# Deformable convolution and attention, fp32, one core: the totals' adds moved two slots forward, the first loads of an image on another queue, and key and query room lent to the last prefetches

## The chip, the cores and the metric

The kernel runs on one core of one Trainium2 chip. A core has five engines with instruction streams of their own, each in order: TensorE (PE; PEld is its weight load), VectorE (DVE), ScalarE (ACT), GpSimd (POOL) and SyncE (SP). Transfers between DRAM and on-chip memory are issued by SyncE, ScalarE and GpSimd, each on a queue of its own, and are carried out by 16 DMA engines that all queues share. The metric is the device time of one execution in microseconds, as the median of several runs. A profiled execution gives the span from its first to its last instruction, and a trace of every instruction.

## The reference

Two layers work on `x` of 2 images x 512 channels x 64 x 64 pixels, all fp32. Layer 0 is a deformable convolution (group norm, offsets and masks, bilinear samples, output projection, residual). It takes the first third of the time, and the change doesn't touch it. Its result `x1` goes into layer 1:

- a group norm of `x1` gives the input of the attention, 4096 pixels of 512 channels per image;
- queries and keys have 64 channels each, q = tanh(Wq x) scaled by a vector, k = tanh(Wk x); values are v = Wv x;
- attention: softmax over all 4096 keys of k.q, for each of 4096 queries; the result is the values' mean under these weights;
- the normalised input is added (a residual inside the attention), the output projection Wfc with bias follows;
- a batch norm over both images and all pixels, with ReLU, and `x1` is added at the end.

Since the batch norm needs the mean and variance of everything, nothing of the output can be stored before the last product is done.

## The kernel before

Layer 1 is written at L1242 to L1807. The order of the instructions on each engine is the order in the code (`tc.manual_schedule()`); no scheduler moves anything.

**Algebra.** Wv and Wfc are merged, so that the values come out already projected. The softmax isn't normalised first: e = exp(scores) is multiplied with the values, all e are summed over the keys ("totals"), and the product is multiplied by the reciprocal of the total at the end. The residual is multiplied by the total beforehand, so that one division serves both. The product of values and e is a two by two block product that uses seven products instead of eight (`ORDER`, L1487), and each of the seven is once more cut in the same way into seven matmuls. So sums and differences of the factors are needed: "forms" of the values (`vform`, `vsum`), made once per image on VectorE, stored to DRAM by SyncE (L1341, L1342) and loaded again as `v`, 448 KB for each slot (L1473); rows of e that become sums of each other (L1387, L1419, L1420); and three block sums `tt` (L1466, L1467) for each slot.

**Loops.** An image has four chunks of 1024 queries (two rows of 512, "row 0" and "row 1"). A chunk has seven products (p), and each sums over nine groups (g): eight groups of 512 keys and a ninth for the residual, whose values are a matrix of weights (`w_d`). One product of one group is a slot: seven block products of two matmuls each. A chunk has 63 slots, numbered l from 0 (p = l // 9, g = l % 9), and an image has 252 (s = 63 k + l).

**Order around a slot.** `slot(s)` issues, in this order: the load of `v` for slot s + 3; `before`, which settles the scores of the slot before (transforms e, adds it to totals) and computes new scores and exponentials that `EVENTS` has for this slot; `at`, with the single events of the slot (loads and normalisations of the residual, at 23 the row sum of row 1's total); the sums `tt` of slot s + 4, with exceptions around 4, 20 and 22; the last adds of a total at slots 4 (row 0) and 22 (row 1); the products; and at the end steps of the work that collects an earlier product. From l = 43 the next chunk's scores are computed beside the products. The scores of the last row piece, `e1`, stand at slots 11, 13, 15 and 20.

**Totals.** Each row has two partial totals of 512 KB. The first e is copied into each by GpSimd's DMA (L1415), later ones are added by accumulating DMAs (L1411), to one and the other in turn (`parts.reverse()`). The last two of row 1, groups 6 and 7, are added by VectorE itself (L1409). `total` then adds the two partial totals (L1436) and folds the sum twice (L1437, L1438), and `spread_total` sums over the partitions on TensorE with a matrix of ones (`pr`, L1442), scales the residual by it (L1458) and copies it to `rin`.

**Start of an image.** For each of the four quarters of an image the keys, queries and values are computed (`values`); row 0's early scores of the first chunk are computed between these (`EARLY`). The forms are stored as they become ready, the last of them during slots 0 to 4 (`step(2)`). The first three loads of `v` are issued behind the third tile of the last quarter, on SyncE's queue, which also carries all stores of the forms.

**Room.** `ring` has 38 pieces of 512 KB for e, totals, pixels, results and prefetches; `wk` has keys (1 MB), queries (512 KB), `rin`, `u`, four `v` and five tiles shared by `tt` and `vsum`. After the loop `wk` is closed and `fin` takes ten pieces in its place.

**The end.** For each of 32 pieces of output (an item), `xr` (the piece of x1) and `cr` (the attention's result, which for the last chunk is kept on chip instead) are loaded; ScalarE applies batch norm and ReLU (L1803), VectorE adds (L1806), GpSimd stores (L1807). From slot 28 of the last chunk GpSimd already prefetches items into free ring pieces; after the loop SyncE fetches five more into `fin`, and the rest follows into pieces that come free, as items are done:

```python
live = 6 + sum(last + g >= l for last in (18, 41, 45, 54) for g in range(NG + 1))
if live + 2 * len(ready) + 2 <= 36:
    fetch(piece, nc.gpsimd)
```

Of the kernel before, what the change touches and what calls it, by code (L numbers as in the profile page):

```python
# [10 lines left out]
F32 = mybir.dt.float32  # L11
# [7 lines left out]
P = 128  # L19
NB = 2  # L20
# [11 lines left out]
CH = 512  # L32
NCH = S // CH
# [494 lines left out]
NG = S // P // 4  # L528
SLOTS = 7 * (NG + 1)
# [45 lines left out]
def window_path(ctx: ExitStack, tc: tile.TileContext, t_in: dict, out: bass.AP, far: bass.AP, sums: bass.AP):  # L575
    nc = tc.nc
# [10 lines left out]
    v_d = [[dram.tile([7, P, 7, P], F32, name=f"wv{n}_{g}") for g in range(NG)] for n in range(NB)]  # L587
    w_d = dram.tile([7, P, 7, P], F32, name="ww")
# [54 lines left out]
    with ExitStack() as l0:  # L643
# [298 lines left out]
        def fetch(i, s):  # L942

            if i >= NSEQ:
                return
            n, ch = divmod(i, NCH)
            t = io.tile([P, PX, C], F32, name="patch", bufs=2)
            for p in range(PX):
                nc.sync.dma_start(
                    t[:SN, p, :], xt_d[n][ch * ROWS + PR * s : ch * ROWS + PR * s + SY, PC * p : PC * p + SX, :]  # L950
                )
            patches[i, s] = t
# [208 lines left out]
        with tc.manual_schedule():  # L1161
# [60 lines left out]
            for i in range(NSEQ):  # L1222
# [6 lines left out]
                w, m, g = Chain(weights, i + 1), Chain(sample, i), Chain(features, i + 3)  # L1229
# [12 lines left out]
    with ExitStack() as l1, tc.manual_schedule():  # L1242
# [9 lines left out]
        def piece(name, shape=(P, 2, CH)):  # L1252
            return ring.tile(list(shape), F32, tag="r", name=name)

        kept = {}
        waiting = deque((n, qb, h) for n in reversed(range(NB)) for qb in range(NCH) for h in range(2))
        ready = deque()

# [10 lines left out]
        with ExitStack() as inner:  # L1269
            wk = inner.enter_context(tc.tile_pool(name="w1work", bufs=1))  # L1270
# [88 lines left out]
                yield  # L1359
                finish(odd, 5, 2)  # L1360

            keys = wk.tile([P, NCH // 2, CH], F32, name="keys")

            def load_queries(n, k):
                q = wk.tile([P, 2, CH], F32, name="q")
                for h in range(2):
                    nc.gpsimd.dma_start(q[h * DQ : (h + 1) * DQ], q_d[n][k])
                return q
# [36 lines left out]
            def add_total(c, qh, t, direct=False):  # L1405
                parts = c.tot.setdefault(qh, [])
                if len(parts) == 2:
                    if direct:
                        nc.vector.tensor_add(parts[0], parts[0], t)  # L1409
                    else:  # L1410
                        nc.gpsimd.dma_start(parts[0], t, accum_op=ALU.add)  # L1411
                    parts.reverse()
                else:
                    parts.append(piece("tot"))
                    nc.gpsimd.dma_start(parts[-1], t)  # L1415
# [15 lines left out]
                    if key == "e1":  # L1431
                        second_row(c, k)

            def total(c, qh):
                t, u = c.tot[qh]
                nc.vector.tensor_add(t, t, u)  # L1436
                nc.vector.tensor_add(t[:, 1, :], t[:, 1, :], t[:, 0, :])  # L1437
                nc.vector.tensor_add(t[:, 1, HQ:], t[:, 1, HQ:], t[:, 0, :HQ])  # L1438

# [27 lines left out]
                nc.vector.tensor_add(t[:, 1:3], t[:, 0].unsqueeze(1).to_broadcast([P, 2, HQ]), x[:, 0:3:2])  # L1467
                return t

            def load_values(n, p, g):  # L1470
                j = PLACE[ORDER[p][1]]
                t = wk.tile([P, 7, P], F32, name="v", bufs=4)
                nc.sync.dma_start(t, v_d[n][g][j] if g < NG else w_d[j])  # L1473
                return t

            def products(c, p, g, v, t):
# [80 lines left out]
            class Attention:  # L1557
# [19 lines left out]

                def fetch(self, s):
                    if s < NCH // 2 * SLOTS:
                        self.v[s] = load_values(self.n, *divmod(s % SLOTS, NG + 1))  # L1580

                def at(self, l, c, s):

# [15 lines left out]
                def slot(self, s):  # L1599
                    k, l = divmod(s, SLOTS)  # L1600
                    c = self.chunks[k]
                    nxt = self.chunks[k + 1] if k + 1 < NCH // 2 else None
                    self.fetch(s + 3)
                    if l % (NG + 1) == 0 and self.ends:
                        next(self.ends[-1], None)
                    self.before(l, c)
                    if nxt and l >= 43:
                        if l == 43:
                            nxt.q = load_queries(self.n, k + 1)
                        self.before(l - SLOTS, nxt)  # L1610
                        self.at(l - SLOTS, nxt, s)
                    self.at(l, c, s)
                    if l == 21:
                        self.sums(s + 3)
                    if l + LEAD not in (8, 24, 26):
                        self.sums(s + LEAD)
                    if l in (4, 22):
                        total(c, int(l > 4))
                    p, g = divmod(l, NG + 1)
                    products(c, p, g, self.v.pop(s), self.t.pop(s))  # L1620
                    for e in self.ends[:-1] if g == 0 else self.ends:
                        next(e, None)
                    if g == NG:
                        self.ends = self.ends[-1:] + [collect(c, p, first_copy(c), c.acc)]
# [75 lines left out]
            for n in range(NB):  # L1700
# [3 lines left out]
                for i in range(NCH // 2):  # L1704
# [22 lines left out]
                    for t in range(4):  # L1727
# [17 lines left out]
                        if t % 2:  # L1745
                            g = 2 * i + t // 2
# [8 lines left out]
                for s in range(NCH // 2 * SLOTS):  # L1755
                    if s == 0:
                        at.at(-7, first, s)
                    if s == 2:
                        at.at(-3, first, s)
                    at.slot(s)  # L1760
                    if s < 5:
                        step(2)
                    if n == 0 and s in (92, 94, 96, 98, 101, 103):
                        next(later, None)
                    l = s - (NCH // 2 - 1) * SLOTS
                    if n + 1 < NB:
                        if l == 47:
                            pixels[0] = load_pixels(n + 1, 0, nc.gpsimd)
                        if l == 49:
                            wc = value_output()  # L1770
                        if l == 51:
                            wcs = sum_value_output(wc)
                        if l in (52, 53):
                            for h in range(2):
                                normalize(pixels[0][l - 52][h], 2 * h, *norms[n + 1])
                        if l == 55:
                            psums[0] = sum_pixels(nc.vector, pixels[0])
                    elif l >= 28 and waiting:
                        live = 6 + sum(last + g >= l for last in (18, 41, 45, 54) for g in range(NG + 1))
                        if live + 2 * len(ready) + 2 <= 36:  # L1780
                            fetch(piece, nc.gpsimd)
                at.rest()

        fin = l1.enter_context(tc.tile_pool(name="w1fin", bufs=10, reuse_waits="tile"))
        for _ in range(5):
            fetch(lambda name: fin.tile([P, 2, CH], F32, tag="f", name=name), nc.sync)
        bmv = bnp.tile([P, KB, 2], F32, name="bmv")
        for kb in range(KB):
# [9 lines left out]
        while ready:  # L1798
            n, qb, h, ct, xr = ready.popleft()
# [61 lines left out]
```

## Time and profile before

| | |
|---|---|
| median of 3 runs | 3458.1 us (3456.04 to 3461.37) |
| profiled execution, its own time | 3457.18 us |
| its span | 3455.3 us, granted TensorE clock 0.968 on average |
| TensorE busy | 3159.9 us (91%) |
| VectorE busy | 2757.1 us (80%) |
| ScalarE, GpSimd busy | 1349.8 us, 432.8 us |
| moved by DMA | 629.99 MB, 182 GB/s on average |
| last product of the attention ends | 3361.8 us |

A group in the profile is named by line, engine and "output tile <- input tiles"; a bracket gives the idle time of the engine just before an instruction and what ended it. In the list of waits a row has the total, the number of times and the longest. Windows give the busy time of each engine in a stretch, with the number of instructions, then TensorE's granted clock, the mean busy share of the 16 DMA engines, and GB/s. A busy TensorE is not always at its full clock; a slot's length shows that better.

### The profile page before, as it was taken

The page shows a single profiled execution, that of the slowest core. Times are in us where ns is not written, and L with a number is a line of the kernel's source. Part 1 is how long each engine was busy: PE and PEld are TensorE (multiplying, and loading weights), DVE is VectorE, ACT ScalarE, POOL GpSimd, SP SyncE. Part 2 cuts the span into 40 slices and gives each one's busy share as a digit, 9 for nine tenths or more (in the row PEclk, how much of TensorE's full clock was granted, in tenths as well). Part 3 has the DMA queues.
Part 4 walks back from the last instruction along what each step waited for, and adds up shares of the span by engine and source line. Part 5 has one row for each costly group of instructions (what it writes and reads, how often), then busy time and mean ns, then how long its engine had stood idle before and what let it go on. Part 6 is the DMA issues. An engine that isn't in the chain of part 4 may idle for free. (4 is left out here: it accounts for less than half of the span.)

```text
span 3455.3 us, 38293 instructions
## 1 busy us (share of the span) xinstructions
PE 3159.9 (91%) x14147; PEld 2270.9 (66%) x14147; DVE 2757.1 (80%) x3826; ACT 1349.8 (39%) x1802; POOL 432.8 (13%) x468
## 2 busy tenths in 40 slices
PE   5789999999999999999999999999899999999990
PEld 2355555555555666687787777887577787787780
DVE  8799999989998577786876867868786786876864
ACT  2477787787776533203113122023212203212105
POOL 2112111211211001001001011001001101001012
PEclk9799999999999999999999999999999999999995
DMA  6333442343233279748557677557857748557679
GB/s 224 103 98 129 130 133 88 114 123 117 89 124 98 95 270 278 229 143 245 179 174 218 180 217 205 180 185 254 252 178 218 209 146 244 170 177 211 216 273 375
DMA packets 238390, 629.99 MB, mean 182 GB/s; under 512 B 28112, under 2 KB 45136, under 8 KB 237168
## 3 DMA queue, kind: packets, MB, share of 16 engines
q1 hardware_dynamic: 184048, 439.72, 38.0%
q0 software_dynamic: 43072, 156.26, 17.6%
q10 hardware_dynamic: 11072, 31.46, 2.6%
q8 instruction: 114, 1.87, 0.2%
q14 instruction: 84, 0.69, 0.1%
HBM read 410.15 MB, written 124.91 MB: 155 GB/s over the span
## 5 line engine op out<-in xcount | busy, mean ns | idle before, releaser
L1487 PE MATMUL accy<-tt,v 128*128 128x256 f32 x2016 | 604.5, 382 | 0.1
L1402 ACT ACTIVATE e<-pS 128x1024 f32<-128x1024 f32 x256 | 248.0, 1021 | 736.0 <-PE pS L1397 727.6
L1487 PE MATMUL accx<-e,v 128*128 128x256 f32 x1792 | 477.6, 389 | 27.1 <-DMA v<-wv 27.1
L1487 PE MATMUL accy<-e,v 128*128 128x256 f32 x1792 | 463.1, 381 | 0.0
L820 DVE SCALAR_TENSOR_TENSOR conv<-xn,L_conv_dw_w_sb,conv 128x504 f32<-128x504 f32 (+1 forms) x512 | 409.3, 807 | 35.5 <-ACT conv L814 21.6
L1487 PEld LDWEIGHTS accx<-e,v 128*128 128x128 f32 x1792 | 335.9, 192 | 148.9 <-issue 83.2
L1487 PEld LDWEIGHTS accy<-tt,v 128*128 128x128 f32 x2016 | 386.5, 192 | 54.1 <-issue 0.5
L1487 PEld LDWEIGHTS accy<-e,v 128*128 128x128 f32 x1792 | 343.9, 192 | 48.1
L1466 DVE TENSOR_TENSOR tt<-e 128x256 f32<-128x256 f32 x448 | 187.8, 419 | 185.4 <-PE accy L1487 158.8
L1467 DVE TENSOR_TENSOR tt<-tt,e 128x512 f32<-128x512 f32 x448 | 310.0, 692 | 15.3
L1487 PE MATMUL accx<-tt,v 128*128 128x256 f32 x1008 | 304.5, 384 | 1.1 <-DVE tt L1466 1.1
L984 PEld LDWEIGHTS pa<-bt,patch 96*128 96x128 f32 x2048 | 250.2, 197 | 57.1 <-issue 34.5
L984 PE MATMUL pa<-bt,patch 96*128 96x128 f32 x2048 | 254.1, 281 | 7.3 <-ACT bt L970 6.4
L970 ACT COPY bt<-pb 96x1024 f32<-96x1024 f32 x124 | 234.6, 2007 | 59.6 <-PE pb L965 57.5
L1397 PE MATMUL pS<-q,keys 64*128 64x512 f32 x1024 | 254.4, 615 | 0.0
L789 PE MATMUL pq<-in_w,xn 128*128 128x512 f32 x512 | 240.1, 613 | 6.9 <-DVE o L882 4.8
L1004 PE MATMUL py<-dT,L_conv_out_w_sb 128*128 128x512 f32 x512 | 234.7, 602 | 4.8 <-ACT dT L995 4.8
L1492 ACT COPY u<-accx 128x256 f32<-128x256 f32 x56 | 20.9, 373 | 531.6 <-PE accx L1487 528.8
L1487 PEld LDWEIGHTS accx<-tt,v 128*128 128x128 f32 x1008 | 194.3, 193 | 28.8 <-DVE tt L1466 1.5
L877 PE MATMUL po<-om_w_pg,feat 128*128 128x432 f32 x512 | 204.7, 545 | 2.5 <-ACT feat L860 2.5
L995 ACT COPY dT<-pa 32x256 f32<-32x256 f32 x496 | 179.9, 363 | 62.5 <-PE pa L984 53.7
L1411 POOL DMA_DIRECT2D tot<-e x144 | 124.0, 885 | 582.0 <-DVE e L1387 277.9
(231 smaller groups left out, 4326.0 us busy)
## 6 DMA issues: line engine op xcount, KB each, us to landing
v<-wv SPq DMA_DIRECT2D x448, 448.0 KB
tot<-e POOLq DMA_DIRECT2D x176, 512.0 KB, 6.9
patch<-xt SPq DMA_DIRECT2D x256, 192.0 KB
v<-ww SPq DMA_DIRECT2D x56, 448.0 KB
wv<-vform SPq DMA_DIRECT2D x48, 512.0 KB
wv<-vsum SPq DMA_DIRECT2D x48, 384.0 KB
xt<-xj SPq DMA_DIRECT2D x128, 128.0 KB
res<-in_x SPq DMA_DIRECT2D x64, 256.0 KB
```

The costliest lines, as they stand in the source:

```text
L789: nc.tensor.matmul(pq, xn[:, kb, 1 + 2 * t : 3 + 2 * t, :].rearrange("p r c -> p (r c)"), in_w[:, kb, :], start=(kb == 0), stop=(kb == KB ...
L820: nc.vector.scalar_tensor_tensor(dst, src, wt, dst, ALU.mult, ALU.add)
L877: nc.tensor.matmul(po[:, : 3 * GP], f[:, kb, t * P : (t + 1) * P], om_w[:, kb].rearrange("p a k g -> p (a k g)"), start=(kb == 0), stop=(k ...
L970: copy(bt[:SN].rearrange("s g q d -> s d (g q)")[:, d0 : d0 + 4, :], pb[:SN])
L984: nc.tensor.matmul(pa[:, p], xp[:SN, p, cb * P : (cb + 1) * P], bt[:SN, 4 * cb : 4 * cb + 4, PX * s + p, :], start=True, stop=True,)
L995: copy(dst, src)
L1004: nc.tensor.matmul(py, out_w[:, kb, cb * P : (cb + 1) * P], dT[:, kb, :], start=(kb == 0), stop=(kb == KB - 1))
L1397: nc.tensor.matmul(p[:, a, :], keys[r, i, (2 * u + h) * P : (2 * u + h + 1) * P], c.q[r, qh, :], start=True, stop=True,)
L1402: nc.scalar.activation(e.rearrange("p a q -> p (a q)"), p.rearrange("p a q -> p (a q)"), AF.Exp)
L1466: nc.vector.tensor_sub(t[:, 0], x[:, 1], x[:, 3])
L1467: nc.vector.tensor_add(t[:, 1:3], t[:, 0].unsqueeze(1).to_broadcast([P, 2, HQ]), x[:, 0:3:2])
L1487: nc.tensor.matmul(out, v[:, blk, :], op, start=(first and g == 0), stop=(final and g == NG))
```

## The change

It has three parts.

1. **Totals.** The add of the two partial totals becomes a function of its own, `merge`. For row 1 it is called at the end of slot 20's preparations, and the two folding adds at slot 21, ahead of the `tt` sums of that slot (before: all three at slot 22, behind `tt` sums of slots 21 and 22). `parts.reverse()` now follows accumulating DMAs only, so both direct adds of groups 6 and 7 go into the first partial total, which already holds the sum. Row 0 keeps its three adds at slot 4.
2. **Loads.** The loads of `v` for the first six slots of each image are issued by ScalarE instead of SyncE. By the order of the code, those of slots 0 to 2 stand on ScalarE behind the early exponentials of the last quarter's third tile, those of slots 3 and 4 ahead of the residual's four normalisations, and that of slot 5 behind them.
3. **Room.** Keys and queries move from `wk` to a pool `lent` that stays to the end. From slot 22 of the last chunk of the last image the room of keys and queries, three pieces, takes prefetches, and the limit counts ring pieces that were really taken instead of two per item. After the loop SyncE fills the ring up to 34 pieces; `fin` has eight pieces instead of ten and takes four items instead of five.

```diff
@@ -1252,7 +1252,12 @@
         def piece(name, shape=(P, 2, CH)):
             return ring.tile(list(shape), F32, tag="r", name=name)
 
-        kept = {}
+        lent = l1.enter_context(tc.tile_pool(name="w1lent", bufs=1))
+        kept, taken = {}, []
+        def ring_piece(name):
+            taken.append(name)
+            return piece(name)
+
         waiting = deque((n, qb, h) for n in reversed(range(NB)) for qb in range(NCH) for h in range(2))
         ready = deque()
 
@@ -1359,10 +1364,16 @@
                 yield
                 finish(odd, 5, 2)
 
-            keys = wk.tile([P, NCH // 2, CH], F32, name="keys")
+            def key_tile():
+                return lent.tile([P, NCH // 2, CH], F32, tag="keys", name="keys")
+
+            def query_tile():
+                return lent.tile([P, 2, CH], F32, tag="q", name="q")
+
+            keys = key_tile()
 
             def load_queries(n, k):
-                q = wk.tile([P, 2, CH], F32, name="q")
+                q = query_tile()
                 for h in range(2):
                     nc.gpsimd.dma_start(q[h * DQ : (h + 1) * DQ], q_d[n][k])
                 return q
@@ -1409,7 +1420,7 @@
                         nc.vector.tensor_add(parts[0], parts[0], t)
                     else:
                         nc.gpsimd.dma_start(parts[0], t, accum_op=ALU.add)
-                    parts.reverse()
+                        parts.reverse()
                 else:
                     parts.append(piece("tot"))
                     nc.gpsimd.dma_start(parts[-1], t)
@@ -1431,9 +1442,12 @@
                     if key == "e1":
                         second_row(c, k)
 
-            def total(c, qh):
+            def merge(c, qh):
                 t, u = c.tot[qh]
                 nc.vector.tensor_add(t, t, u)
+
+            def total(c, qh):
+                t = c.tot[qh][0]
                 nc.vector.tensor_add(t[:, 1, :], t[:, 1, :], t[:, 0, :])
                 nc.vector.tensor_add(t[:, 1, HQ:], t[:, 1, HQ:], t[:, 0, :HQ])
 
@@ -1467,10 +1481,10 @@
                 nc.vector.tensor_add(t[:, 1:3], t[:, 0].unsqueeze(1).to_broadcast([P, 2, HQ]), x[:, 0:3:2])
                 return t
 
-            def load_values(n, p, g):
+            def load_values(n, p, g, queue):
                 j = PLACE[ORDER[p][1]]
                 t = wk.tile([P, 7, P], F32, name="v", bufs=4)
-                nc.sync.dma_start(t, v_d[n][g][j] if g < NG else w_d[j])
+                queue.dma_start(t, v_d[n][g][j] if g < NG else w_d[j])
                 return t
 
             def products(c, p, g, v, t):
@@ -1577,7 +1591,9 @@
 
                 def fetch(self, s):
                     if s < NCH // 2 * SLOTS:
-                        self.v[s] = load_values(self.n, *divmod(s % SLOTS, NG + 1))
+                        self.v[s] = load_values(
+                            self.n, *divmod(s % SLOTS, NG + 1), nc.scalar if s < 6 else nc.sync
+                        )
 
                 def at(self, l, c, s):
 
@@ -1610,12 +1626,16 @@
                         self.before(l - SLOTS, nxt)
                         self.at(l - SLOTS, nxt, s)
                     self.at(l, c, s)
+                    if l == 20:
+                        merge(c, 1)
                     if l == 21:
+                        total(c, 1)
                         self.sums(s + 3)
                     if l + LEAD not in (8, 24, 26):
                         self.sums(s + LEAD)
-                    if l in (4, 22):
-                        total(c, int(l > 4))
+                    if l == 4:
+                        merge(c, 0)
+                        total(c, 0)
                     p, g = divmod(l, NG + 1)
                     products(c, p, g, self.v.pop(s), self.t.pop(s))
                     for e in self.ends[:-1] if g == 0 else self.ends:
@@ -1775,14 +1795,20 @@
                                 normalize(pixels[0][l - 52][h], 2 * h, *norms[n + 1])
                         if l == 55:
                             psums[0] = sum_pixels(nc.vector, pixels[0])
-                    elif l >= 28 and waiting:
+                    elif l >= 22:
+                        if l == 22:
+                            room = key_tile()
+                            spare = deque((room[:, 0:2], room[:, 2:4], query_tile()))
                         live = 6 + sum(last + g >= l for last in (18, 41, 45, 54) for g in range(NG + 1))
-                        if live + 2 * len(ready) + 2 <= 36:
-                            fetch(piece, nc.gpsimd)
+                        if len(spare) > 1 or live + len(taken) + 2 <= 36:
+                            fetch(lambda name: spare.popleft() if spare else ring_piece(name), nc.gpsimd)
                 at.rest()
-
-        fin = l1.enter_context(tc.tile_pool(name="w1fin", bufs=10, reuse_waits="tile"))
-        for _ in range(5):
+                if n + 1 == NB:
+                    while len(taken) + 2 <= 34:
+                        fetch(ring_piece, nc.sync)
+
+        fin = l1.enter_context(tc.tile_pool(name="w1fin", bufs=8, reuse_waits="tile"))
+        for _ in range(4):
             fetch(lambda name: fin.tile([P, 2, CH], F32, tag="f", name=name), nc.sync)
         bmv = bnp.tile([P, KB, 2], F32, name="bmv")
         for kb in range(KB):
```

## The prediction

> **What bounds the kernel now.** The profiled execution took 3457.2 us, of which 3455.3 are its span; the 1.9 us around the span I leave unchanged. I read the page's busy shares first, then TensorE's list of waits (which wait ends last before the busiest engine), then timelines around those waits, then the windows of the end. The page's chain was of no use: it lists 0% for everything.
>
> ```profile
> PE 3159.9 (91%) x14147; PEld 2270.9 (66%) x14147; DVE 2757.1 (80%) x3826; ACT 1349.8 (39%) x1802; POOL 432.8 (13%) x468
> PE pr L1442 <- DVE tot L1438: 31.5, 8, 3.9
> ...
> PE accx L1487 <- DMA v<-wv: 27.1, 5, 12.4
> ```
>
> TensorE is busy for 91%, so in the attention only its gaps and the end, where it does nothing, can be won. Between 1360 and 3362 us the gaps over 0.3 us are these two rows and one of 1.1 us. The first is the sum over rows in every chunk (eight chunks). VectorE's and TensorE's timelines at the first:
>
> ```profile
> 1456.62 1.22 DVE L1525 TENSOR_TENSOR ct<-ct 128x1024 f32<-128x1024 f32 x1
> 1460.74 0.43 DVE L1387 TENSOR_TENSOR e<-e 128x256 f32<-128x256 f32 x1 [2.91 <-ACT e L1402]
> ...
> 1467.83 1.22 DVE L1409 TENSOR_TENSOR tot<-tot,e 128x1024 f32<-128x1024 f32 x1
> 1468.98 0.42 DVE L1466 TENSOR_TENSOR tt<-e 128x256 f32<-128x256 f32 x1
> ...
> 1471.10 1.22 DVE L1436 TENSOR_TENSOR tot<-tot 128x1024 f32<-128x1024 f32 x1
> 1472.35 0.69 DVE L1437 TENSOR_TENSOR tot<-tot 128x512 f32<-128x512 f32 x1
> 1473.08 0.42 DVE L1438 TENSOR_TENSOR tot<-tot 128x256 f32<-128x256 f32 x1
> ```
> ```profile
> 1473.65 1.10 PE L1442 MATMUL pr<-tot,ones_k 128*128 128x512 f32 x2 [3.94 <-DVE tot L1438]
> 1474.58 1.87 PE L1487 MATMUL accx<-e,v 128*128 128x256 f32 x4
> ...
> 1479.29 1.03 PE L1487 MATMUL accx<-e,v 128*128 128x256 f32 x4
> ```
>
> VectorE stands 2.91 us idle before the last scores, and then has more to do than fits before TensorE wants the totals. The gap also has an echo. An undisturbed slot lasts 3.02 us from start to start; the one after the gap lasts 1479.29 − 1474.58 = 4.71, because its matmuls take twice as long (four in 1.87 us, not 1.03) at a granted clock of 0.50 to 0.65 from 1474 to 1478. That is 1.69 us more, in six of the eight chunks. In the chunk at 2169 the echo is absent; in that at 3005 it is 0.9 (in the row sum) + 1.63.
>
> The second row, at the start of each image: a wait of 12.39 us for forms of the values, while the DMA engines are full.
>
> ```profile
> 2458.87 2.07 PE L1487 MATMUL accx<-e,v 128*128 128x256 f32 x4 [12.39 <-DMA v<-wv]
> 2455.18 0.43 DVE L1466 TENSOR_TENSOR tt<-e 128x256 f32<-128x256 f32 x1 [4.52 <-DMA wv<-vsum]
> q0 software_dynamic: 863, 3.15, 72.6%
> q1 hardware_dynamic: 1122, 2.12, 33.0%
> ```
>
> The last two lines are packets, MB and share of the DMA engines from 2443 to 2461 us: together above 100%. VectorE waits for a store there at the same time. And the end, windows with busy times, clock, DMA share and GB/s:
>
> ```profile
> 3362.00:3376.00 14.00, 0.56 (x3) 0.19 (x3) 11.32 (x26) 7.39 (x11) 1.25 (x3) 0.63 0.81 277
> 3376.00:3449.00 73.00, 0.00 (x0) 0.00 (x0) 36.66 (x30) 41.69 (x58) 22.55 (x31) 0.50 1.01 407
> ```
>
> From 3376 on nothing but the DMA engines is full: 407 GB/s for 73 us.
>
> [...] from 2455 to 2457 us 80 packets of each of the two queues ran. [...]
>
> **Part 1, totals.** Now slot 22 runs two pairs of `tt` sums (1468.98 to 1471.10, 2.12 us) and three adds (to 1473.5). The change puts the first add (merge, 1.22, 1.25 with its issue) at slot 20, behind the add that ends at 1457.84, and the two others ahead of the `tt` sums. So 1.25 + 2.12 = 3.37 us leave the path from the last L1409 to the row sum: the gap of 3.94 becomes 0.57. Too short for the echo: the gaps of about 1 us at 2433 and 2435 had none. What hides the merge is the idle 2.91; without that cover it costs 1.25. It adds a wait: both partial totals must have their accumulating DMAs (L1411) landed. Queued behind it are the settling of the last scores, their totals and TensorE's row sum. I matched each chunk's last accumulation with the end of L1525: landed at 1459.36 against 1457.84, then 1690.98/1689.62, 1922.26/1921.85, 2155.12/2153.63, and in the second image 0.0 to 0.4 before it. The latest start is 1.52 after L1525, 1.52 + 1.25 = 2.77 < 2.91: nothing late in any chunk, with 0.1 to 0.2 us to spare in the tightest two. The second direct add goes to the same tile as the first; it costs the same 1.22. The `tt` pairs run 1.1 us later (0.69 + 0.42); they feed slots 24 and 25, past two slots of 3 us. The scaling of the residual (L1458) starts 2.6 us earlier, and the sum that needs it has, by my count, 1.1 us left. Row 0's total, at slot 4, keeps its three adds in place. Sum: 6 × (3.94 − 0.57 + 1.69) = 30.4; the 2169 chunk 3.37; the 3005 chunk 3.37 + 0.90 + 1.63 = 5.9. Together **39.7**.
>
> **Part 2, first loads on ScalarE.** Per image six of SyncE's loads of 448 KB (12 issues) move; SyncE loses those, ScalarE gains them. The order of instructions puts the first three behind the last early exponentials, two ahead of the residual's normalisations and one behind them; behind these stand the exponentials of slots 4 and later. Seen alone this could save up to the 27.1 + echoes, but TensorE meets the next wait: VectorE's `tt` sums stand behind stores of `vsum` (4.52, 1.87 and 5.63 in the second image; 9.72 and 3.18 in the first), and from there it works without a break to the first row's total, at 1400.1 and 2466.8, which TensorE's row sum at 1401.6 and 2469.9 needs. So only 1.3 + 2.9 = 4.2 can come off. On the other side the loads now compete with the stores that they stood behind. The stores at 2435.17 landed at 2455.2; if the fourth and fifth load (0.92 MB) take their turn first at the 118 GB/s that SyncE's queue had (2.12 MB in 18 us), the stores land 7.8 later; 9.5 with an echo, 19 for both images. [...] Bounds −19 and +4.2; I take **−2**.
>
> **Part 3, the end.** Keys and queries move to a pool of their own; its 3 pieces of 512 KB take prefetches from slot 22 of the last chunk, and the ring is counted by what is really taken. By the order of instructions GpSimd fetches 32 pieces in the loop (26 before), SyncE 12 after it (8), and the recycled ones fall from 26 to 16. Six pieces are thus loaded while TensorE works. There the DMA has moved 416 GB/s (3320 to 3340) with no wait of TensorE, and the forms are loaded three slots (9 us) ahead: I cost it at nothing; uncovered it is 6 × 1.25 = 7.5. A piece of 524 KB takes 1.25 us at 0.42 MB/us. After the loop the DMA moves 12 + 16 + 32 stores = 60 pieces instead of 58 in the full window and some more before 3376, 64 with all of the 8. Of the 8, three were issued at 3350, before TensorE had finished, and of the 12 none may be. 60 pieces are 75 us; started between 3363 and 3367 as the ring comes free, with 1 us for the last store, they end at 3439 to 3443, where stores now end at 3448.5. Gain 5 to 10, I take **7.5**.
>
> **Sum.** 39.7 − 2 + 7.5 = 45.2. The profiled execution goes from 3457.2 to 3412.0; the median is 3458.1, 0.9 above it, so 3413.
>
> **Rivals.**
> A, as above, 3413.
> B, the stores don't suffer: TensorE gets the 4.2 and an echo or two of 1.7: 3403 to 3407. For it speaks that on ScalarE's ring no store stands ahead of the loads, as four or more do on SyncE's; against it that VectorE's chain behind the stores stays.
> C, the third queue starves the stores at the start of the images: −12 to −19 instead of −2: 3423 to 3430. For it speaks the wait of VectorE on stores that already sets the start[...].
> D, the end gains 0 to 2, because SyncE's first ring load waits for a piece that is free only after 3367 and the loads of the other pool stand behind it: 3418 to 3421.
> E, the other side: the merge waits for its accumulations. GpSimd's DMAs land 2.9 to 11.9 us after issue (median 8.6, total tiles from 1240 to 1480 us). Each microsecond beyond the 1.66 that the idle time covers delays the row sum. The gain of 45 is eaten when all eight wait 45.2 / 8 = 5.6 us longer: landings 7.3 after L1525, where the trace has 1.5 at most. From there it is slower, at 6.5 us 3465.
> That the change does nothing is out: the adds' order has changed on VectorE, and nothing else holds the totals up.
>
> **Chances.** A 0.60, B 0.13, C 0.13, D 0.08, E (with unknown stalls of the same size) 0.06. The range from 3399 to 3431 takes in A, B, D and most of C. A time within 0.2% (7 us) can't be told from no change. Faster 0.93, within it 0.02 (between C and E lies little), slower 0.05: E, of which a sixth falls within.
>
> **What would show it.** Part 1: the row TensorE `pr` behind the totals falls from 31.5 to about 5, no slot of 4.7 us after it, L1438 follows L1409 directly, the merge lies in the 2.9 us idle; wrong if VectorE shows a wait of the merge for `tot<-e`. Part 2: the wait for `v` shrinks and the same time turns up as a wait of TensorE for `tt` or for the totals of row 0 within the first six slots; wrong to the good if the first six slots of an image end over 4 us sooner after its last values matmul; wrong to the bad if VectorE's waits for `vsum` stores grow beyond 24.9. Part 3: the full DMA window ends 5 to 10 us sooner after TensorE's last product (86.7 us now, 3361.8 to 3448.5), with 16 recycled loads; wrong if it starts later or a wait for `v` appears after slot 22 of the last chunk.

## The result, and the profile after

The kernel after takes 3409.26 us (median of 4 runs, 3408.64 to 3413.08), the kernel before 3457.07 in the runs beside it: a ratio of 0.9863, 95% interval 0.9845 to 0.9880. That is 47.8 us less, where 45.2 was forecast. The profiled execution took 3413.1 us, with a span of 3411.3: the slowest of the four, and 44.0 under the span before. One of the six executions of the experiment `room` below took 12083.14 us, at a granted clock of 0.371, and is left out of its comparison. The difference of the spans can be laid out by milestones that both traces have (starts of matmuls, in us):

| stretch | before | after | difference |
|---|---|---|---|
| start to layer 1's first matmul (untouched) | 1218.9 | 1219.7 | +0.8 |
| last values matmul to slot 9, first image | 57.1 | 57.1 | 0.0 |
| the same, second image | 56.7 | 56.7 | 0.0 |
| slot 20 to slot 30, sum over eight chunks | 295.5 | 257.6 | −37.9 |
| the rest of the chunks, up to the last product | | | +3.1 |
| end of the last product to the end of the span | 93.5 | 83.5 | −9.9 |

So the totals brought what they were to bring, the loads nothing at all, and the end more than I had it down for. The lists of waits of TensorE and VectorE in the profile after (microseconds in total, times, longest):

```profile
PE pS L1408 <- ACT e L1413: 15.3, 2, 7.8
PE pr L1456 <- DVE tot L1452: 13.6, 12, 3.0
...
PE accx L1501 <- DVE tt L1480: 5.1, 3, 2.2
```
```profile
DVE tt L1480 <- DMA wv<-vsum: 26.4, 8, 5.4
...
DVE tot L1447 <- DMA tot<-e: 19.1, 9, 4.7
```

The 27.1 us of waiting for `v` are gone from the first list, and the row sum's 31.5 are 13.6, of which 5.6 are row 0's at the start of the images (2.52 and 3.03) and 1.5 row 0's of a later chunk. New is a wait of 15.3 for the exponentials of slot 4, once in each image. Around the row sum of the second chunk, VectorE's timeline and TensorE's read now

```profile
1684.85 1.22 DVE L1539 TENSOR_TENSOR ct<-ct 128x1024 f32<-128x1024 f32 x1
1685.98 1.22 DVE L1447 TENSOR_TENSOR tot<-tot 128x1024 f32<-128x1024 f32 x1
1688.97 0.43 DVE L1398 TENSOR_TENSOR e<-e 128x256 f32<-128x256 f32 x1 [1.77 <-ACT e L1413]
...
1696.06 1.23 DVE L1420 TENSOR_TENSOR tot<-tot,e 128x1024 f32<-128x1024 f32 x1
1697.32 0.69 DVE L1451 TENSOR_TENSOR tot<-tot 128x512 f32<-128x512 f32 x1
1698.05 0.42 DVE L1452 TENSOR_TENSOR tot<-tot 128x256 f32<-128x256 f32 x1
```
```profile
1698.62 1.10 PE L1456 MATMUL pr<-tot,ones_k 128*128 128x512 f32 x2 [0.68 <-DVE tot L1452]
1699.55 1.03 PE L1501 MATMUL accx<-e,v 128*128 128x256 f32 x4
...
1702.58 0.59 PE L1501 MATMUL accx<-e,v 128*128 128x256 f32 x2
```

The merge (L1447) lies inside what was 2.91 us of idle time, of which 1.77 are left; the two folds stand right behind the last direct add. The gap is 0.68, and the next slot takes 1702.58 − 1699.55 = 3.03 us: no echo. In the first chunk it is not so smooth. There the merge waits for its accumulations, the last of which lands at 1460.92 in the trace (the bracket names no transfer), starts at 1461.00, and the gap is 1.29:

```profile
1461.00 1.23 DVE L1447 TENSOR_TENSOR tot<-tot 128x1024 f32<-128x1024 f32 x1 [2.39 <-issue]
```

The end, in windows that begin 0.2 us after the last product as those before did (busy times, clock, DMA share, GB/s):

```profile
3328.00:3342.00 14.00, 0.56 (x3) 0.19 (x3) 11.32 (x26) 7.41 (x11) 1.25 (x4) 0.59 0.69 241
3342.00:3405.00 63.00, 0.00 (x0) 0.00 (x0) 36.63 (x30) 40.96 (x58) 22.48 (x31) 0.50 1.03 416
3405.00:3411.20 6.20, 0.00 (x0) 0.00 (x0) 0.00 (x0) 0.00 (x0) 0.00 (x0) 0.50 0.17 69
```

The full window is 63 us long instead of 73. Length times GB/s, summed over the three windows, is 30.0 MB; before it was 34.2 MB (88 GB/s in the last 7 us). The difference is about 8 pieces of 524 KB.

### The profile page after: what moved, and what is told of

Its sections match the earlier page's. It is cut to its first block, busy times and chain, and to the rows that moved or that the text cites. A ratio compares the mean times of both kernels' runs of the same rounds, so it can differ in the third digit from the quotient of the medians.

```text
span 3411.3 us, 38291 instructions
## 1 busy us (share of the span) xinstructions
PE 3152.2 (92%) x14147; PEld 2265.2 (66%) x14147; DVE 2755.0 (81%) x3826; ACT 1349.5 (40%) x1802; POOL 435.7 (13%) x474
## 3 DMA queue, kind: packets, MB, share of 16 engines
q10 hardware_dynamic: 12800, 36.97, 3.0%
## 5 line engine op out<-in xcount | busy, mean ns | idle before, releaser
L820 DVE SCALAR_TENSOR_TENSOR conv<-xn,L_conv_dw_w_sb,conv 128x504 f32<-128x504 f32 (+1 forms) x512 | 409.4, 808 | 37.5 <-ACT conv L814 23.6
L1481 DVE TENSOR_TENSOR tt<-tt,e 128x512 f32<-128x512 f32 x448 | 310.0, 692 | 15.3
L1408 PE MATMUL pS<-q,keys 64*128 64x512 f32 x1024 | 257.9, 623 | 15.3 <-ACT e L1413 15.3
L995 ACT COPY dT<-pa 32x256 f32<-32x256 f32 x496 | 179.6, 362 | 66.0 <-PE pa L984 56.7
```

Of the source, the lines that this page charges most:

```text
L820: nc.vector.scalar_tensor_tensor(dst, src, wt, dst, ALU.mult, ALU.add)
L995: copy(dst, src)
L1408: nc.tensor.matmul(p[:, a, :], keys[r, i, (2 * u + h) * P : (2 * u + h + 1) * P], c.q[r, qh, :], start=True, stop=True,)
```

## The experiments

The kernel before ran beside each group and took 3456.87, 3457.48 and 3460.08 us in the medians. Layer 0, which no kernel here touches, takes between 1213 and 1220 us to layer 1's first matmul in the profiled executions, so a difference of a few us between two medians says little; the traces are compared from that matmul on. The starts of the images vary too. Where the code of the start is that of the kernel before (`before`, `totals`, `room`), slot 9 comes 57.1 to 58.7 us after the last values matmul in the first image and 53.2 to 56.7 in the second; where it is that of the kernel after (`after`, `loads`, `folds_late`, `merge_early`, `no_fill`), 56.7 to 57.7 and 54.6 to 56.7.

### The three parts, one at a time

**totals**: part 1 alone, the core of its edit

```diff
+                    if l == 20:
+                        merge(c, 1)
                     if l == 21:
+                        total(c, 1)
                         self.sums(s + 3)
```

> The kernel before with part 1 alone. My prediction: 39.7 us faster. What the trace after suggests instead: 35 us faster (about 4.95 us in each chunk between slots 20 and 30, less where the merge waits for its accumulations, and some 3 us given back at the totals of row 0). Rival: part of the measured 48 us belongs to the loads, and this gives under 30.

Measured: 3418.86 us, ratio 0.9889 (0.9875 to 0.9904), 38 us faster than before. Its trace has slots 20 to 30 37.6 us shorter in sum. So part 1 is nearly all of the gain in the attention; the rival is out.

**loads**: part 2 alone

```diff
-                nc.sync.dma_start(t, v_d[n][g][j] if g < NG else w_d[j])
+                queue.dma_start(t, v_d[n][g][j] if g < NG else w_d[j])
...
+                            self.n, *divmod(s % SLOTS, NG + 1), nc.scalar if s < 6 else nc.sync
```

> The kernel before with part 2 alone. My theory: 0, within 4 us: TensorE's wait for v (27.1 us) goes, and as much comes back as waits for the exponentials and for the total of row 0, so that slot 9 of each image starts at the same time after the last values matmul (57.1 and 56.7 us). Rival B: 6 to 10 us faster. Rival C: 10 to 19 us slower.

Measured: 3456.30 us, ratio 0.9999 (0.9991 to 1.0007). TensorE's wait for `v` is gone, and three others stand in its place; those of the second image in its timeline:

```profile
2439.38 0.70 PE L1487 MATMUL accx<-tt,v 128*128 128x256 f32 x2 [2.18 <-DVE tt L1466]
2461.96 3.78 PE L1397 MATMUL pS<-q,keys 64*128 64x512 f32 x8 [8.53 <-ACT e L1402]
2471.76 1.10 PE L1442 MATMUL pr<-tot,ones_k 128*128 128x512 f32 x2 [2.59 <-DVE tot L1438]
```

They add up to 13.3 us, where the waits for `v` and `tt` had 14.5, and slot 9 comes 56.5 us after the last values matmul (57.3 in the first image). VectorE's wait for stores of `vsum` is 26.3 us, against 24.9 before. Both rivals, B and C, are out.

**room**: part 3 alone

```diff
+                        if len(spare) > 1 or live + len(taken) + 2 <= 36:
+                            fetch(lambda name: spare.popleft() if spare else ring_piece(name), nc.gpsimd)
...
+                    while len(taken) + 2 <= 34:
+                        fetch(ring_piece, nc.sync)
```

> The kernel before with part 3 alone. By the pieces that are still to be moved after the last product (56 instead of 63, 1.25 us each): 8.75 us faster; by the trace after: 9.9. My prediction had 7.5. Rival D: 0 to 2.

Measured: 3447.74 us with the long execution, 3447.23 without it: 9.6 us faster by the medians. The ratio of 0.9964 (0.9951 to 0.9977) stands for 12 us, between 8 and 17. In its trace the end takes 83.4 us from the last product, 10.1 less. The count of 63 pieces in what I expected was two too low; that is worked out under part 3 below. By the medians the three parts give 38.0 + 0.6 + 9.6 = 48.2, and all of them together 47.8: no sign that they act on each other, but each of these numbers is only known to some us.

### What the totals' gain is made of

**folds_late**: in the kernel after, the two folds go back to slot 22

```diff
                     if l == 21:
-                        total(c, 1)
                         self.sums(s + 3)
...
+                    if l == 22:
+                        total(c, 1)
```

> The kernel after with row 1's two folding adds back at slot 22, behind the tt sums; the merge stays at slot 20. The gap before the row sum grows by 2.12 us (two pairs of tt sums), from 0.68 to 2.8 in each of eight chunks. If a gap of this length brings no slow slot after it: 17 us slower than the kernel after. If it does bring the echo of 1.69 us each time: 30 us slower.

Measured: 3431.00 us, 21.7 us slower than the kernel after, between the two values. The gap is 2.67 to 2.78 us in all eight chunks. Two rows of TensorE's timeline from the first chunk, then three from the third:

```profile
1474.00 1.10 PE L1456 MATMUL pr<-tot,ones_k 128*128 128x512 f32 x2 [2.68 <-DVE tot L1452]
1474.93 1.03 PE L1501 MATMUL accx<-e,v 128*128 128x256 f32 x4
...
1932.40 1.10 PE L1456 MATMUL pr<-tot,ones_k 128*128 128x512 f32 x2 [2.67 <-DVE tot L1452]
1933.33 1.45 PE L1501 MATMUL accx<-e,v 128*128 128x256 f32 x4
1934.57 1.06 PE L1501 MATMUL accx<-tt,v 128*128 128x256 f32 x2
```

The same gap leaves the first chunk's matmuls at their 1.03 us and doubles those of the third (two `tt` matmuls in 1.06, not 0.59). Two of eight chunks have the echo, of 1.69 and 1.5 us. So a gap of 3.94 is followed by slow matmuls in seven of eight chunks (22 of 24 with the traces of `loads` and `room`), one of 2.7 in two of eight, one of up to 1.3 in none. I had expected no echo behind the short gap because two gaps of about 1 us in the trace before had none; the counts bear that out up to 1.29. Why gaps of one length end in slow matmuls in some chunks and not in others, no run here shows. Slots 20 to 30 are 18.4 us longer in sum than in the kernel after: 2.0 × 8 for the gaps and 3.2 for the two echoes, less the 0.8 that the first and the third chunk had lost already.

**merge_early**: in the kernel after, row 1's merge goes to slot 17

```diff
-                    if l == 20:
+                    if l == 17:
                         merge(c, 1)
```

> The kernel after with row 1's merge at slot 17 instead of 20: rival E's mechanism on purpose. At slot 17 VectorE is ready for it at about 1451 us in the first chunk, the last accumulations land at about 1459. If E's price is right, the wait of about 8 us, less the 2.9 us of idle time at slot 20, delays the row sum in every chunk: a gap of 5 to 7 us before it, with an echo of 1.7 in most: 45 to 65 us slower than the kernel after, so no faster than the kernel before. If VectorE makes the time up by slot 22, within 5 us of the kernel after.

Measured: 3452.96 us, ratio to before 0.9988 (0.9981 to 0.9995): 43.7 us slower than the kernel after, more than the 38.0 that part 1 had gained. The size is just under what rival E's price gave; the place is another. VectorE's and TensorE's timelines in the first chunk, and the row of TensorE's list of waits:

```profile
1455.98 1.23 DVE L1447 TENSOR_TENSOR tot<-tot 128x1024 f32<-128x1024 f32 x1 [7.54 <-DMA tot<-e]
...
1458.19 0.68 DVE L1530 TENSOR_TENSOR ct<-u,accx 128x512 f32<-128x512 f32 x1
```
```profile
1458.92 1.13 PE L1408 MATMUL pS<-q,keys 64*128 64x512 f32 x4 [2.29 <-DVE ct L1530]
...
1460.98 2.08 PE L1408 MATMUL pS<-q,keys 64*128 64x512 f32 x4 [0.93 <-DVE ct L1533]
...
PE pS L1408 <- DVE ct L1530: 22.5, 8, 4.1
```

Behind the merge's 7.54 us stands the collecting of the finished product (L1530), which empties the tiles that the scores of slot 20 are to be written to (the wait of 2.29 for `ct`). TensorE so stops before the row sum is even near: slot 19 takes 9.55 us instead of 5.03 in the first chunk, 9.1 to 11.2 in all. The eight slots 19 are 40.1 us longer in sum, which is nearly the whole loss; 22.5 us of that are the waits in this row of the list, and shorter waits and slow matmuls follow them. I had named the settling of scores and the row sum behind the wait, and not this.

### Why the loads bring nothing

The rows of **loads** name two waits that follow each other: ScalarE's exponentials stand behind normalisations that wait for the residual's load, and the row sum of slot 5 behind VectorE's wait for stores. Three edits at the start of an image take these away one after another, and a fourth puts the loads back on SyncE.

**norm_late**: the kernel after with row 0's normalisations at slot 5

```diff
-                    if s == 2:
+                    if s == 5:
                         at.at(-3, first, s)
```

> The second edit alone. If both waits bind together: 0 to 3 us faster than the kernel after; TensorE's wait for exponentials at slot 4 (15.3 us in two) goes and comes back before the row sum of slot 5. If ScalarE's wait alone binds: as much as both edits together.

**vsum_room**: the kernel after with `vsum` of the last two groups in ring pieces

```diff
-                            fill.append(filling(*raw, v_d[n][g], piece if g + 1 == NG else None))
+                            fill.append(filling(*raw, v_d[n][g], piece if g + 2 >= NG else None))
```

> The first of those two edits alone. If both waits bind together: 0 to 5 us faster than the kernel after, because ScalarE's exponentials at slot 4 still wait for the residual. If VectorE's wait for stores alone binds: as much as both edits together.

**start_both**: both of these edits.

> The kernel after with two more edits at the start of an image: vsum of the last two groups in ring pieces (tt sums no longer wait for stores), and the residual's normalisations of row 0 at slot 5 instead of 2 (exponentials no longer wait for the residual's load). My theory, that VectorE's chain behind the stores and ScalarE's wait for the residual bind the first nine slots together: 8 to 20 us faster than the kernel after, slot 9 at under 52 us after the last values matmul. Rival: the full DMA engines bind, and it is the same within 4 us.

**start_three**: both, and the last form's steps behind slot 4 and not behind slot 3

```diff
-                    if s < 5:
+                    if s < 3 or s == 4:
                         step(2)
```

> Both edits at the start of an image and a third: the last form's steps (L1363, L1341, L1342) move from behind slot 3 to behind slot 4, so that row 0's total no longer stands behind their wait for a store, and the load of v for slot 7 no longer stands behind their stores. If VectorE's order behind the stores sets slot 5's row sum, that sum comes some 10 us sooner (37.5 us after the last values matmul in the run without the third edit), and the kernel is 10 to 24 us faster than the kernel after. Rival: the accumulations or the loads of v land late too, as the DMA engines are full until 35 us after it: then within 5 us of the kernel after.

**vsum_steps**: the edits of `vsum_room` and of `start_three`'s diff, without that of `norm_late`.

> As the first of this group but with the residual's normalisations left at slot 2. If ScalarE's wait for the residual's load counts once the chain is relieved: slower than with all three edits, by 2 to 10 us; otherwise the same.

**three_sync**: `start_three` with part 2 of the change undone

```diff
-                            self.n, *divmod(s % SLOTS, NG + 1), nc.scalar if s < 6 else nc.sync
+                            self.n, *divmod(s % SLOTS, NG + 1), nc.sync
```

> The same with all loads of v back on SyncE's queue, part 2 of the change undone. If part 2 gained nothing only because VectorE's chain hid it, it counts here: 5 to 15 us slower than with it. If the DMA engines bind anyway: the same within 4 us.

Measured, with the starts in us after the last values matmul, first image / second image, and VectorE's or TensorE's wait that stands last before the row sum:

| kernel | median, ratio to before | slot 4 | row sum, slot 5 | slot 9 | last wait |
|---|---|---|---|---|---|
| before | 3457.07 | 36.8 / 36.4 | 39.9 / 39.5 | 57.1 / 56.7 | `v` |
| loads | 3456.30, 0.9999 | 32.3 / 31.5 | 38.4 / 37.5 | 57.3 / 56.5 | `vsum` store |
| after | 3409.26, 0.9863 | 32.1 / 31.4 | 38.2 / 37.7 | 57.1 / 56.7 | `vsum` store |
| norm_late | 3414.76, 0.9875 | 23.2 / 22.4 | 38.8 / 38.4 | 58.9 / 57.3 | `vsum` store |
| vsum_room | 3403.84, 0.9844 | 32.2 / 30.2 | 36.9 / 36.6 | 54.2 / 55.5 | exponentials, `vform` store |
| start_both | 3410.16, 0.9861 | 26.9 / 26.3 | 37.5 / 37.5 | 56.7 / 56.5 | `vform` store |
| start_three | 3405.05, 0.9846 | 26.7 / 26.7 | 35.9 / 36.4 | 55.9 / 56.2 | accumulations |
| vsum_steps | 3402.82, 0.9835 | 32.2 / 31.2 | 36.3 / 35.4 | 54.3 / 53.5 | exponentials, accumulations |
| three_sync | 3408.33, 0.9854 | 40.0 / 33.7 | 43.1 / 36.9 | 60.3 / 54.0 | `v`, accumulations |

The row sum hardly moves, whatever is taken from in front of it, and the table's last column changes instead. In `norm_late` slot 4 starts 9 us sooner than in the kernel after, and TensorE then stands in front of the row sum:

```profile
1400.55 2.04 PE L1456 MATMUL pr<-tot,ones_k 128*128 128x512 f32 x2 [12.28 <-DVE tot L1452]
```

In `start_both` VectorE no longer waits for stores of `vsum`, but for the store of a form that it is to overwrite (L1363, three instructions ahead of the totals):

```profile
1392.85 1.22 DVE L1363 TENSOR_TENSOR vform<-vform 128x1024 f32<-128x1024 f32 x1 [9.42 <-DMA wv<-vform]
```

In `start_three`, with the total moved ahead of that, it waits as long for the accumulations into the total:

```profile
1390.49 1.23 DVE L1447 TENSOR_TENSOR tot<-tot 128x1024 f32<-128x1024 f32 x1 [10.35 <-DMA tot<-e]
```

And in `three_sync`, with the loads back on SyncE, the wait for `v` is there again:

```profile
1392.24 2.08 PE L1501 MATMUL accx<-e,v 128*128 128x256 f32 x4 [11.88 <-DMA v<-wv]
```

Four different transfers end last in turn, between 26 and 34 us after the last values matmul. In `norm_late`, as in the kernel after, VectorE then works for 12 us without a break up to the row sum, so there its own work is what binds. As this work is moved away, the next transfer lands later: the store that `start_both` waits for at 33 us, the accumulations of `start_three` at 33 to 34. What these transfers share is the DMA engines. Windows of `start_both` at the second image's start, whose last values matmul ends at 2412.0:

```profile
2412.00:2420.00 8.00, 3.00 (x13) 1.31 (x12) 4.95 (x9) 1.94 (x2) 0.61 (x1) 0.94 1.05 313
...
2430.00:2440.00 10.00, 10.00 (x46) 7.41 (x45) 4.37 (x10) 3.78 (x5) 1.34 (x2) 1.00 1.04 338
2440.00:2450.00 10.00, 2.13 (x9) 1.60 (x8) 5.24 (x8) 2.34 (x4) 0.00 (x0) 0.81 1.05 346
2450.00:2460.00 10.00, 10.00 (x37) 6.56 (x36) 7.06 (x13) 2.53 (x3) 0.00 (x0) 0.84 0.51 190
```

They are full (a DMA share of 1.04 to 1.06) until about 2450, some 38 us after that matmul, and the row sum comes when they are done, 37.5 us after it. In the 34 us after it the kernels before and after both have a share of 1.05, at 309 and 315 GB/s. My theory for this group, that two waits of the engines bind together, fell: `start_both` was to be 8 to 20 us faster and is the same. The rival, the full DMA engines, fits the kernels in which VectorE's chain is relieved; in the others that chain and the transfers end at about the same time. It is inferred from windows and from waits that replace each other; a kernel that moves fewer bytes at this point wasn't tried, so that a part of it may still be the order in which the transfers are served. Nor did any experiment touch GpSimd's queue, accumulations and loads of the residual above all, which had 72.6% of the DMA engines' time in the window of the kernel before that the prediction shows.

Against what was expected, by the medians: `norm_late` was to gain up to 3 us on the kernel after and is 5.5 slower, though the two intervals overlap. `vsum_room` gains 5.4 where up to 5 was said. `start_three` gains 4.2, as its rival had it (within 5), and not 10 to 24. `vsum_steps` isn't slower than `start_three`, so ScalarE's wait for the residual shows no cost. `three_sync` is 3.3 us slower than `start_three`, within the 4 that the full DMA engines allowed, which doesn't show part 2 to be worth more once the chain is relieved. What differs between these kernels is the length of TensorE's last gap before the row sum (3.1 us in `vsum_room`, 12.65 in `norm_late`, second image) and the slow matmuls behind it; that this makes their times wasn't tried. `vsum_room` and `vsum_steps` reach slot 9 1.2 to 3.2 us sooner than the kernel after; in the first image that is beyond the spread given above, in the second `vsum_room` lies within it. With 3402.82 us, ratio 0.9835 (0.9820 to 0.9850), `vsum_steps` has the lowest median of all. It is clear of the kernel before; its interval overlaps that of the kernel after (0.9845 to 0.9880).

### The end

**no_fill**: the kernel after without the filling of the ring behind the loop

```diff
-                    while len(taken) + 2 <= 34:
-                        fetch(ring_piece, nc.sync)
```

> The kernel after without the filling of the ring by SyncE at the end of the loop: two items, four pieces fewer are loaded before the last product, and come as recycled ones instead. At 1.25 us a piece in a window where only the DMA engines are full: 5 us slower than the kernel after. If the end is set by something else (the first output, ScalarE, SyncE's wait for the other pool): within 1 us of it.

Measured: 3415.14 us, 5.9 us slower than the kernel after; the end takes 88.8 us instead of 83.5, so 5.3 more for four pieces, 1.33 each. The window of full DMA is as full as in the kernel after (1.02 and 1.03), and 5.5 us longer:

```profile
3337.94:3406.44 68.50, 0.00 (x0) 0.00 (x0) 36.63 (x30) 41.27 (x58) 22.49 (x31) 0.50 1.02 415
```

## Why the prediction was right, point by point

**Part 1, right; the sum was 5 us too large.** Forecast 39.7, and the trace has 37.9 between slots 20 and 30 and 34.8 over whole chunks. The step from 3.94 to a short gap, and the echo that goes with it, came as worked out: 4.95 us a chunk in most, where 3.37 + 1.69 = 5.06 was said, because the gap left is 0.68 and not 0.57. Two terms were mis-sized. "Nothing late in any chunk" was wrong for the first and the third: with landings that differ from those of before, the merge waited 2.39 and 1.97 us, and as 1.25 had to follow inside 2.91, the row sum was 0.6 and 0.2 late. I had 0.1 to 0.2 us to spare there and treated that as enough, although each landing was seen only once. The other is 3.1 us that my sum did not have at all: 1.75 before a row sum of row 0 at 2910, whose total the change left in place, 0.5 before another at 2085, and 0.9 at 1741, where TensorE waited for a collecting step. Row 0's total waits for its accumulations in both kernels (up to 2.85 us before, 4.73 after), and in `totals` it costs 1.7 in another chunk, at 3128. A part of the 5 us is also the trace that I had: the echoes behind the gap of 3.94 vary, and in `loads` and `room`, whose totals are those of the kernel before, slots 20 to 30 sum up to 298.6 and 298.5 us, 3 more than in `before`.

**Part 2, right in the chain that binds and within its bounds.** I took −2, with bounds of −19 and +4.2; `loads` is 0.6 us faster by the medians, with an interval from 3.1 faster to 2.4 slower. The next wait was there as said, VectorE's stores, with VectorE at work without a break from the last of them to the row sum of slot 5. That row sum came 1.7 us sooner, out of at most 4.2, and lost it again: in the kernel after TensorE takes 5.74 us from it to the scores of slot 6, against 3.97 before, as slow matmuls follow the gaps ahead of it (7.5 and 3.0 us in the second image). The −2 was my estimate for stores that suffer, and they hardly did: VectorE's waits for them are 26.4 us, where `before`, `room` and `totals` have 24.9, 23.5 and 22.5. For an estimate so far from the −19 I had 80 packets of each of two queues in 2 us; this shows that the two queues shared the engines there, and not how a third would fare beside them. Two things I did not see. The larger of the new waits, 15.3 us for the exponentials of slot 4, I had not named; `norm_late` shows that it doesn't set the row sum. And other transfers stand right behind VectorE's chain, so that relieving the chain brings little as well.

**Part 3, right; undersized by a quarter.** 7.5 forecast, 9.9 measured. The price of a piece stood the test: 1.25 said, 1.33 in `no_fill`. The count did not. I had 64 pieces after the loop before and 60 after. The first was a slip, as 8 + 26 + 32 are 66. Of SyncE's eight before, moreover, one was issued while TensorE still worked and not three: I had read this row as three loads at 3350,

```profile
3350.09 12.51 SPq L1262 DMA_DIRECT2D xr<-wx  x3
```

but it lasts 12.51 us, and the second and third load were issued at 3361.81 and 3362.18, after the last product (3361.78). So 65 pieces were left. In the kernel after, four of SyncE's twelve were issued while TensorE still worked:

```profile
3318.34 0.32 SPq L1267 DMA_DIRECT2D xr<-wx  x1
...
3327.36 0.32 SPq L1271 DMA_DIRECT2D cr<-wc  x1
3332.21 0.32 SPq L1267 DMA_DIRECT2D xr<-wx  x1
```

I had said that none may be. The ring's pieces come free from slot to slot up to the last product at 3327.76, and 65 pieces became 56. Nine pieces at 1.25 are 11.3 us. Rival D's wait is there as well: the fifth load, the first into the other pool, is issued 4.5 us after the last product, when VectorE has read `rin` for the last time (L1511 ends at 3332.2), and seven loads stand behind it. It costs DMA share (0.69 in the first 14 us, 0.81 before), by an estimate from these shares 14 × 0.12 = 1.7 us of the 11.3, and did not eat the gain: 9.6 would be left, and 9.9 were measured.

**The sum.** 39.7 − 2 + 7.5 = 45.2 against 34.8 + 0 + 9.9, less 0.8 that layer 0 took longer in this execution: 43.9 between the spans, 47.8 between the medians. Two errors of 5 and 2.4 with opposite signs, and 2 for part 2, made the sum better than its terms. That the total came within 3 us is luck to this extent.

## What to carry to other kernels

A gap on the busiest engine is to be priced with what follows it: here a wait of 3.94 us cost 5.6, because slow matmuls came behind it, and none came behind the gaps of 0.68 to 1.29 us that took its place. Where the DMA engines are full, as at the start of these images (a share of 1.05), moving a transfer to another queue may only change which wait comes last; look at the DMA share of the stretch, and at the work behind the transfer, before pricing a wait for one of them. A row of a timeline that holds several instructions gives the start of the first alone. And work that is moved into idle time has to be compared with the spread of what it waits for, not with one landing that the trace happens to show.

## What the runs showed of the hardware

Before the row sum of row 1, a gap of 2.67 to 2.78 us in the stream of matmuls was followed by slow matmuls in two of eight places (`folds_late`), one of 3.94 us in 22 of 24 (`before`, `loads`, `room`), gaps of 0.68 to 1.29 us in none of eight (the kernel after). The twelve loads that ScalarE issues ran on another queue than the stores of the forms: q10 has 12800 packets and 36.97 MB in the kernel after, and 11072 and 31.46 before. In its window from 2414 to 2448 us, with a DMA share of 1.05, the packets of q0, q1 and q10 took 53.9%, 30.9% and 20.1% of the engines' time. The stores lost little by it: VectorE waited 25.2 to 26.4 us for stores of `vsum` with the loads on a third queue (`merge_early`, `loads`, the kernel after), and 22.5 to 24.9 with them on the stores' own (`totals`, `room`, before).
